# A dense mixture of experts rewritten as a sorted one: every token sent to bins in HBM, 46 slots of 128 rows, answers scattered back

## The chip, the cores and the metric

The kernel runs on one core of one Trainium2 chip. The metric is the device time of one execution in microseconds (us). The kernel before takes 582.26 us, the median of 3 runs.

## The reference

The input is 8 sequences of 256 tokens with 128 features, all float32. Four layers follow each other, and each ends in a residual and a layer norm:

```python
x = _layernorm(x + _L0_attn_ref(x, ...))   # 16 heads, weights (qk)^2-like (a Taylor kernel), causal
x = _layernorm(x + _L0_ffn_ref(x, ...))    # top 1 of 2 experts plus a shared one, hidden 512
x = _layernorm(x + _L1_attn_ref(x, ...))   # 16 heads of 8 with rotary positions, causal softmax
x = _layernorm(x + _L1_ffn_ref(x, ...))    # top 2 of 8 experts, hidden 256
```

The last one is what the change is about:

```python
scores = einsum('bsd,ed->bse', x, Wg)
topk_scores, topk_idx = top_k(scores, 2)
topk_probs = softmax(topk_scores)
h1 = einsum('bsd,efd->bsef', x, W1); h2 = einsum('bsd,efd->bsef', x, W2)
expert_out = einsum('bsef,edf->bsed', silu(h1) * h2, W3)     # all 8 experts for all tokens
out = sum over the two chosen e of topk_probs * expert_out
```

The reference computes all 8 experts for every token and uses two of them.

## The kernel before, in words

Nothing is written in the order in which it runs. The code calls `add` for each operation (a few instructions with the engines that could do them, an estimated cost, and the buffers read and written); `Plan.order` then places all operations by a list schedule with these costs, and the engines' instruction streams follow that order. Each engine works through its own stream in order and waits on semaphores for the others.

The work is cut into stages. `attention0` (stage a) and `attention1` (stage b) run once for each of the 8 sequences, `ffn0` (stage f) and `ffn1` (stage h) once for each of 4 pairs of sequences, 512 tokens. `LIMIT` bounds how many stages of a kind may be open at once, and `STEP`, `LATER`, `WEIGHT` and `WINDOW` set the priorities. All matmuls go through the helper `mm`, so they carry its line, L334, and all copies that of `copy` (L338 on ACT, L340 on DVE).

PSUM has 8 banks: one tile `S` of 4 banks, and 4 single ones. `attention1` fills `S` six times for each sequence: three times with scores whose maximum DVE takes (L982), three times with scores that ACT raises to the exponent (L1028); each filling waits until the one before it has been read. POOL's causal select (L1038) then clears the upper triangle, before the matmuls of attend.

`ffn1` handles 512 tokens with all experts. DVE ranks the 8 gate scores of each token and forms the two gates; they are turned and spread over the partitions (L1183), and the input is multiplied by the gate of each expert (L1189). Then follow 16 chunks (8 experts, two halves of the hidden width): up1, `silu` on ACT (L1208), up2 on the gated input, a product on DVE (L1221), and down into one accumulator. Each chunk has 2 matmuls of 512 columns and 4 of 128. The expert weights `e1`, `e2`, `e3`, 3 MB, are loaded once. The stage ends with a residual (L1238), `layernorm` (L490) and a store by SP.

`layernorm` takes statistics on DVE (L498, L500), the root by a logarithm and an exponential on ACT (L507, L515), and two normalizing operations on POOL or DVE (L522).

Of the kernel before, what the change touches and what calls it, by code (L numbers as in the profile page):

```python
# [10 lines left out]
F32 = mybir.dt.float32  # L11
BF16 = mybir.dt.bfloat16
AF = mybir.ActivationFunctionType
# [3 lines left out]
P = 128  # L17
# [7 lines left out]
E, F = 8, 256  # L25
NEG = -1e30
# [7 lines left out]
for table, parts in (  # L34
# [11 lines left out]
            ("sel8", 1024),  # L46
# [10 lines left out]
def shape_constants():  # L57
# [40 lines left out]
    for j in range(E):  # L98
        part(b, CB, "sel8")[p % 32 == j, 128 * j : 128 * j + 128] = 1.0
# [3 lines left out]
class Buf:  # L103
    def __init__(self, kind, size, name):
        self.kind, self.size, self.name = kind, size, name
        self.slot = None
        self.left = 0
        self.free_at = 0.0
# [9 lines left out]
class Plan:  # L118
# [35 lines left out]
    def order(self, weigh, window=0.12):  # L154
# [8 lines left out]
        slots = {k: [0.0] * n for k, n in self.slots.items()}  # L163
        heap = np.zeros(self.heap)
# [10 lines left out]
        def earliest(b):  # L175
            if b.kind == "heap":
                return room(b.size).min()
            return min(min(slots[k]) for k in b.kind)

        def take(b, t):  # L180
            if b.kind == "heap":
                fit = np.flatnonzero(room(b.size) <= t + 1e-9)
                b.slot = int(fit[0] if b.size > 2 else fit[-1])
                heap[b.slot : b.slot + b.size] = math.inf
                known.clear()
                return
# [6 lines left out]
        def give(b):  # L193
            if b.kind == "heap":
                heap[b.slot : b.slot + b.size] = b.free_at
                known.clear()
            else:
# [83 lines left out]
SLOTS = {"S": 1, "bank": 2, "acc": 2, "vz": 2, "mx": 2, "g4": 2, "small": 40}  # L281
LIMIT = {"a": 4, "f": 4, "b": 2, "h": 3}
HEAP = 160
STEP = {"a": 20.02, "f": 13.515, "b": 17.177, "h": 3.607}
LATER = {"a": -58.15, "f": 14.456, "b": -40.963, "h": 225.772}
WEIGHT = 2.1411
WINDOW = 0.0441
# [3 lines left out]
def network(  # L291
    ctx: ExitStack, tc: tile.TileContext, x, xT, wqk, wv, wo, small, b2, w1, w2, wqkv, wo1,
    e1, e2, e3, ca, cb, out,
# [3 lines left out]
    psum = ctx.enter_context(tc.tile_pool(name="psum", bufs=1, space=bass.MemoryType.PSUM))  # L297
    ctx.enter_context(tc.manual_schedule())

    def fixed(name, shape, dtype=F32):  # L300
        return pool_.tile(shape, dtype, tag=name, name=name)

    banks = [psum.tile([P, 512], F32, tag=f"b{i}", name=f"b{i}") for i in range(4)]
    heap = fixed("heap", [P, HEAP * 256])
    tiles = {
        "S": [psum.tile([P, 4, 512], F32, tag="S", name="S")],
        "bank": banks[2:],
        "acc": banks[:2],
        "vz": [fixed(f"vz_{i}", [P, 1280]) for i in range(SLOTS["vz"])],
        "mx": [fixed(f"mx_{i}", [P, 2, P]) for i in range(SLOTS["mx"])],  # L310
        "g4": [fixed(f"g4_{i}", [P, 4, P]) for i in range(SLOTS["g4"])],
# [3 lines left out]
    def ap(b):  # L315
        if b.kind == "heap":
            return heap[:, b.slot * 256 : (b.slot + b.size) * 256]
        return tiles[b.slot[0]][b.slot[1]]
# [5 lines left out]
    SIZES = {"k8": 8, "k6": 6, "k4": 4, "k2": 2, "k1": 1}  # L324

    def buf(kind, name):
        if kind in SIZES:
            return Buf("heap", SIZES[kind], name)
        if kind == "bank":
            return Buf(("bank", "acc"), 1, name)  # L330
# [140 lines left out]
    for kind, width in (("vz", 1280), ("mx", 256), ("g4", 512)):  # L471
# [18 lines left out]
    def layernorm(tag, r, kind="k1"):  # L490
# [29 lines left out]
        for t in range(2):  # L520
            def apply(e, t=t):
                ENG[e].tensor_scalar(  # L522
                    ap(y)[:, t * P : (t + 1) * P],
# [332 lines left out]

    def attention1(s, xi):
# [240 lines left out]
        return layernorm(f"b{s}", r)  # L1100
# [3 lines left out]
    def ffn1(g, xs):  # L1104
        pt = buf("bank", f"pth{g}")
        xT_ = buf("k2", f"xTh{g}")
        add(f"turn h{g}", pe1(512), transposes(pt, xs), r=both(xs[0]) + both(xs[1]) + ["ca"], w=[pt])
        add(f"turned h{g}", act(512) + dve(512), lambda e: copy(e, ap(xT_), ap(pt)), r=[pt], w=[xT_])
        pg = buf("bank", f"pe{g}")

        def scores(e):
            for t in range(4):
# [5 lines left out]
        add(f"gates {g}", pe(512), scores, r=[xT_, "sml"], w=[pg])  # L1118
        sb = buf("small", f"gs{g}")
        v3 = lambda b, n=E: ap(b)[:, 0 : 4 * n].rearrange("p (t e) -> p t e", t=4)  # L1120
        add(f"gs {g}", act(32) + dve(32), lambda e: copy(e, ap(sb), ap(pg)[:, 0:32]), r=[pg], w=[sb])
        shape = [P, 4, E, E]
        gt, ge = buf("k1", f"gt{g}"), buf("k1", f"ge{g}")
        v4 = lambda b: ap(b).rearrange("p (t a b) -> p t a b", t=4, a=E)
        other = lambda: v3(sb).unsqueeze(2).broadcast_to(shape)
        own = lambda: v3(sb).unsqueeze(3).broadcast_to(shape)
        add(f"gt {g}", dve(256), lambda e: nc.vector.tensor_tensor(v4(gt), other(), own(), ALU.is_gt), r=[sb], w=[gt])
        add(f"ge {g}", dve(256), lambda e: nc.vector.tensor_tensor(v4(ge), other(), own(), ALU.is_ge), r=[sb], w=[ge])
        add(
            f"ge2 {g}", dve(256) + pool(256, True),  # L1130
            lambda e: ENG[e].tensor_mul(
                ap(ge).rearrange("p (t c) -> p t c", t=4),
                ap(ge).rearrange("p (t c) -> p t c", t=4),
                kb("tri8").unsqueeze(1).broadcast_to([P, 4, E * E]),
# [3 lines left out]
        add(f"beats {g}", dve(256), lambda e: nc.vector.tensor_max(ap(gt), ap(gt), ap(ge)), r=[ge], w=[gt])  # L1138
        rank, top, ex, num, den = (buf("small", f"{n}{g}") for n in ("rank", "top", "ex", "num", "den"))
        add(f"rank {g}", dve(256), lambda e: nc.vector.tensor_reduce(v3(rank), v4(gt), AX.X, ALU.add), r=[gt], w=[rank])  # L1140
        add(f"top {g}", dve(32), lambda e: nc.vector.tensor_reduce(v3(top, 1), v3(sb), AX.X, ALU.max), r=[sb], w=[top])
        add(
            f"less {g}", dve(32),
# [221 lines left out]
```

## Time and profile before

| | before |
|---|---|
| median of 3 runs | 582.26 us (580.42 to 582.88) |
| the profiled execution: its time, its span | 582.61 us, 580.9 us |
| instructions in the span | 11773 |
| PE busy | 566.1 us, 97% |
| DVE, ACT, POOL busy | 347.7, 285.4, 80.0 us |
| DMA | 11.99 MB, mean 21 GB/s |

The profile is of one execution. Span is the time from the first to the last instruction. In the groups, a line reads: code line, engine, operation, output and input with their partitions and shape, number of records; then busy time in us and mean ns of one; then the engine's idle time ahead of them and what ended it. A rounded row of digits gives the busy share in tenths in 40 equal slices of the span. PE is TensorE, DVE VectorE, POOL GpSimd, SP the queue that issues DMAs.

### The profile page before, as it was taken

To read this page: it belongs to the slowest core of one execution; us is meant where nothing else is said; L and a number is where in the kernel's file an instruction comes from. 1 tells how busy PE (TensorE), PEld (TensorE's weight loads), DVE (VectorE), ACT (ScalarE), POOL (GpSimd) and SP (SyncE) were. 2 spreads that over 40 slices of the span, in tenths; PEclk is the share of its full clock that TensorE was granted. 3 is DMA by queue.
4 is the path that set the end of the run, shared out by engine and by line. 5 is a ranking of instruction groups with operands and counts; after the bars stand their busy time and mean duration, and the time that the engine had idled before them with its cause. 6 is when DMAs were issued, how large, how long until landed. Compare 5 with 4: busy or idle time off the path is not lost.

```text
span 580.9 us, 11773 instructions
## 1 busy us (share of the span) xinstructions
PE 566.1 (97%) x5146; PEld 370.4 (64%) x5146; DVE 347.7 (60%) x602; ACT 285.4 (49%) x402; POOL 80.0 (14%) x79
## 2 busy tenths in 40 slices
PE   6999999999999999999999999999999999999995
PEld 3666675676666766776666764565565555666674
DVE  2767557655525872777685799757894433513625
ACT  2765666665546535362536358634555322545112
POOL 3000100100000401140424060310301100000100
PEclk9999999999999999999999999999999999999999
DMA  7600000000230000000000000000000000000001
GB/s 279 204 5 1 3 1 1 1 1 1 91 128 2 2 1 2 1 1 3 2 1 2 1 2 3 0 2 1 1 1 1 2 0 0 20 1 1 18 1 37
DMA packets 7433, 11.99 MB, mean 21 GB/s; under 512 B 723, under 2 KB 6102, under 8 KB 6870
## 3 DMA queue, kind: packets, MB, share of 16 engines
q1 hardware_dynamic: 7382, 11.24, 5.7%
q8 instruction: 40, 0.66, 0.5%
q14 instruction: 11, 0.09, 0.1%
HBM read 10.19 MB, written 1.05 MB: 19 GB/s over the span
## 4 chain that ended last, share of the span: by engine, by line
PE 91%; DVE 4%; issue 2%; ACT 1%; POOL 1%; DMA 1%; SPq 0%; DVEq 0%; ACTq 0%; POOLq 0%
PE b L334 73%; PE S L334 17%; PE b L486 1%; DVE heap L910 1%; DMA heap<-in_wqk 1%; ACT L1287 0%; ACT heap L1208 0%; DVE mx L982 0%; DVE heap L876 0%; DVE heap L920 0%; POOL heap L897 0%; DVE heap L1138 0%; DVE heap L522 0%; DVE heap L1221 0%; POOL heap L522 0%
## 5 line engine op out<-in xcount | busy, mean ns | idle before, releaser
L334 PE MATMUL b<-heap 128*128 128x128 f32 (+4 forms) x2272 | 422.4, 358 | 5.3 <-DMA heap<-in_wqk 4.3
L334 PEld LDWEIGHTS b<-heap 128*128 128x128 f32 (+1 forms) x2272 | 267.0, 179 | 127.9 <-issue 82.7
L334 PE MATMUL S<-heap 32*128 32x256 f32 (+1 forms) x1536 | 86.1, 346 | 0.7 <-ACT heap L338 0.7
L334 PEld LDWEIGHTS S<-heap 32*128 32x128 f32 x1536 | 62.4, 186 | 37.5 <-issue 10.0
L1208 ACT ACTIVATE heap<-b 128x512 f32<-128x512 f32 x64 | 37.2, 597 | 88.9 <-PE b L334 88.7
L1221 DVE TENSOR_TENSOR heap<-b,heap 128x512 f32<-128x512 f32 x64 | 43.7, 688 | 60.6 <-PE b L334 60.5
L982 DVE TENSOR_REDUCE mx<-S 128x8 f32<-128x2048 f32 (+1 forms) x24 | 55.0, 2291 | 24.5 <-PE S L334 24.4
L522 POOL TENSOR_SCALAR heap<-heap,sm,sm 128x128 f32<-128x128 f32 x21 | 20.5, 981 | 319.5 <-ACT sm L515 195.1
L338 ACT COPY heap<-b 128x512 f32<-128x512 f32 (+1 forms) x63 | 36.1, 572 | 56.2 <-PE b L334 44.7
L612 ACT ACTIVATE heap<-S,rt_half 128x1536 f32<-128x1536 f32 x32 | 49.2, 1537 | 19.8 <-PE S L334 19.7
L825 ACT ACTIVATE heap<-b,sml 128x512 f32<-128x512 f32 x41 | 28.2, 687 | 60.9 <-PE b L334 60.2
L1028 ACT ACTIVATE heap<-S 128x2048 f32<-128x2048 f32 x24 | 45.1, 1877 | 26.6 <-PE S L334 26.6
L621 DVE SCALAR_TENSOR_TENSOR heap<-heap,ca 128x1024 f32<-128x1024 f32 x32 | 39.1, 1222 | 24.1 <-ACT heap L612 23.1
L1038 POOL TENSOR_SCALAR_AFFINE_SELECT heap<-heap 128x1024 f32<-128x1024 f32 (+1 forms) x24 | 36.8, 1532 | 102.4 <-ACT heap L1028 102.4
L340 DVE COPY heap<-b 128x512 f32<-128x512 f32 (+1 forms) x29 | 18.9, 653 | 37.6 <-PE b L334 26.1
L1287 ACT ACT_TABLE_LOAD x24 | 30.8, 1283 | 0.4
L334 PE MATMUL b<-heap,vz 128*32 128x128 f32 (+1 forms) x512 | 25.8, 330 | 0.9 <-POOL heap L1038 0.6
L733 DVE TENSOR_TENSOR heap<-heap,S 128x1024 f32<-128x1024 f32 x16 | 18.9, 1216 | 5.8 <-PE S L334 5.8
L334 PEld LDWEIGHTS b<-heap,vz 128*32 128x32 f32 x512 | 13.3, 109 | 14.2 <-issue 5.1
L1189 DVE TENSOR_TENSOR heap<-S,heap 128x2048 f32<-128x2048 f32 x8 | 18.3, 2282 | 4.2 <-PE S L334 4.2
L671 ACT ACTIVATE heap<-heap 128x512 f32<-128x512 f32 x28 | 17.6, 630 | 1.5 <-DVE heap L340 0.6
L522 DVE TENSOR_SCALAR heap<-heap,sm,sm 128x128 f32<-128x128 f32 x43 | 14.6, 375 | 5.6 <-ACT sm L515 5.4
(93 smaller groups left out, 315.3 us busy)
## 6 DMA issues: line engine op xcount, KB each, us to landing
heap<-in_e SPq DMA_DIRECT2D x3, 1024.0 KB, 5.9
heap<-in_w SPq DMA_DIRECT2D x2, 768.0 KB, 6.1
cb<-in_cb SPq DMA_DIRECT2D x1, 1332.0 KB, 8.0
heap<-in_xT SPq DMA_DIRECT2D x8, 128.0 KB, 3.2
heap<-in_x SPq DMA_DIRECT2D x8, 128.0 KB, 3.2
out<-heap SPq DMA_DIRECT2D x8, 128.0 KB, 1.9
heap<-in_wv SPq DMA_DIRECT2D x1, 512.0 KB
heap<-in_wo SPq DMA_DIRECT2D x1, 512.0 KB, 5.2
```

The lines of the kernel that those rows point to most:

```text
L334: nc.tensor.matmul(o, l, r, start=start, stop=stop, skip_group_check=True)
L338: nc.scalar.copy(o, i)
L522: ENG[e].tensor_scalar(ap(y)[:, t * P : (t + 1) * P], ap(r)[:, t * P : (t + 1) * P], ap(mv)[:, 2 * t : 2 * t + 1], ap(rs)[:, 2 + t : 3 + t ...
L612: lambda e, sc=sc, atv=atv: nc.scalar.activation(atv(), ap(sc)[:, :, 0:384], AF.Square, bias=rt_half, scale=SQ_SCALE),
L621: lambda e, atv=atv: nc.vector.scalar_tensor_tensor(atv()[:, :, 0:256], atv()[:, :, 0:256], 0.5, ka("tri").unsqueeze(1).broadcast_to([P, 4 ...
L825: nc.scalar.activation(ap(h), ap(ph), AF.Relu, bias=bias)
L982: nc.vector.tensor_reduce(ap(mx)[:, min(part, 1), :].rearrange("p (i j r) -> p i j r", j=4, r=8)[:, :, lo : lo + n, 0], ap(sc).rearrange(" ...
L1028: lambda e, sc=sc, pr=pr: nc.scalar.activation(ap(pr).rearrange("p (i c) -> p i c", i=4), ap(sc), AF.Exp),
L1038: nc.gpsimd.affine_select(out=d, in_=d, compare_op=ALU.is_ge, fill=0.0, base=0, pattern=[[0, 4 * n], [1, P]], channel_multiplier=-1,)
L1208: lambda e, pa=pa, sl=sl: nc.scalar.activation(ap(sl), ap(pa), AF.Silu),
L1221: lambda e, pb_=pb_, sl=sl, h=h: nc.vector.tensor_mul(ap(h), ap(pb_), ap(sl)),
L1287: nc.scalar.preload_act_table_set(table[state])
```

## The change

The second expert network computes only the chosen experts. Stage h is gone, and three new ones stand in its place.

- `route` (stage r, once for each sequence): ranks the gate scores as before, and counts with small bf16 matmuls at which place of which expert's bin each token belongs. `twice` doubles the row, and each copy gets its gate and the number of the row that its answer belongs to (130 columns in all). Four indirect DMAs of POOL (`scatter`) send 128 rows each into bins in HBM. A bin has room for every token.
- `listed` (once for each of two groups of sequences, 0 to 5 and 6 to 7): makes, from the counts, a list of slots. A slot is a tile of 128 rows of one expert. As the counts are known only at run time, there are as many slots as could be needed: 31 for group 0, 15 for group 1.
- `slot` (stage s, 46 times): SP reads two values of the list from SBUF into a register and fetches 128 rows of a bin and the 393 KB of that expert's weights from a table in HBM; PE turns the rows, and up, `silu`, product, down follow for 128 rows; the answer is multiplied by the gate, and one indirect DMA of POOL (`put`) sends the 128 answers to their places. Rows of a bin that hold no token carry numbers of rows that nobody reads.
- `combine` (stage c, once for each sequence): loads the two answers of each token, adds them and the residual, and ends as before.

The bins, 9.5 MB, are cleared at the start by 11 DMAs of SP, with row numbers written by POOL. The PSUM tiles may be shared more freely (`PLACES`: `S` takes banks 0 to 3, kind `any` any of the 8), and the planner's constants are new.

In the built order, attention0 of all sequences stands first, then ffn0 with attention1, then the rest of attention1, and the slots last: the first slot's transpose stands on PE behind the last matmul of attention1 (`wo1` of sequence 7), with the routing of sequence 7 between the first slots. ffn0's last matmul stands ahead of two of the three exponent parts of sequence 4, all three of sequence 5, and all of sequences 6 and 7. On SP all 46 fetches stand ahead of the loads of answers and of the stores; on POOL the scatters stand among the causal selects and the puts behind nearly all of these.

```diff
+GROUPS = ((0, 1, 2, 3, 4, 5), (6, 7))
+ROWS = [len(g) * T for g in GROUPS]
+TILES = [r // P for r in ROWS]
+SLOTN = [2 * t + E - 1 for t in TILES]
+XW = D + 2
...
-SLOTS = {"S": 1, "bank": 2, "acc": 2, "vz": 2, "mx": 2, "g4": 2, "small": 40}
-LIMIT = {"a": 4, "f": 4, "b": 2, "h": 3}
+PLACES = {"S": (0,), "acc": (4, 5), "bank": (4, 5, 6, 7), "any": range(8)}
+SLOTS = {"vz": 2, "mx": 2, "small": 60}
+LIMIT = {"a": 4, "f": 3, "b": 3, "r": 3, "s": 8, "c": 8}
...
-STEP = {"a": 20.02, "f": 13.515, "b": 17.177, "h": 3.607}
-LATER = {"a": -58.15, "f": 14.456, "b": -40.963, "h": 225.772}
-WEIGHT = 2.1411
-WINDOW = 0.0441
+STEP = {"a": 13.636, "f": 36.493, "b": 17.344, "r": 67.492, "s": 2.885, "c": 0}
+LATER = {"a": -290.559, "f": 14.115, "b": -656.553, "r": 89.828, "s": 48.725, "c": 674.472}
+WEIGHT = 2.8227
+WINDOW = 0.0366
...
-    def ffn1(g, xs):
...
+            add(
+                f"clear {g}{a}", [("SP", 0.2 * w, 0.2 * w + 3.0)],
+                lambda e, rows_=rows_, g=g, a=a, w=w: nc.sync.dma_start(
+                    bins[g][a * P : (a + w) * P, :].rearrange("(j p) c -> p j c", p=P),
+                    rows_()[:, 0:w, :],
+                ),
...
+    def route(g, i, st):
...
+        def places(e):
+            o, c = ap(pc), chosen()
+            mm(o[:, 0:16], strict_bf, c, True, False)
+            mm(o[:, 8:16], ones_bf, c[:, 0:8], False, False)
+            mm(o[:, 16:24], ones_bf, c[:, 0:8], False, False)
+            mm(o[:, 16:24], ones_bf, c[:, 8:16], False, True)
...
+                    f"scatter {s}{t}{k}", [("POOL", 1.2, 4.0)],
+                    lambda e, t=t, k=k, n=n: nc.gpsimd.indirect_dma_start(
+                        bin_views[g][n][:, :],
+                        bass.IndirectOffsetOnAxis(
+                            ap=ap(idx)[:, 2 * k + t : 2 * k + t + 1].bitcast(I32), axis=0
+                        ),
+                        rows4(st)[:, t, k, :], None,
+                    ),
+                    r=[(idx, 0), *both(st), (st, "gate"), (st, "dest"), (st, "twice"), *cleared[g]],
...
+    def slot(g, n):
+        tag = f"{g}.{n}"
+        xs_, ws = buf("k1", f"sx{tag}"), buf("k3", f"sw{tag}")
+
+        def fetch(e):
+            rows = ap(lists[g]).bitcast(I32)
+            v = nc.sync.value_load(rows[0:1, n : n + 1], min_val=0, max_val=bins[g].shape[0] - P)
+            nc.sync.dma_start(ap(xs_)[:, 0:XW], bins[g][bass.ds(v, P), :])
+            v = nc.sync.value_load(rows[0:1, 32 + n : 33 + n], min_val=0, max_val=(E - 1) * P)
+            nc.sync.dma_start(ap(ws)[:, 0 : 6 * P], wtab[bass.ds(v, P), :])
+
+        add(
+            f"fetch {tag}", [("SP", 2.0, 5.0)], fetch,
+            r=[lists[g], (lists[g], 1), *scattered[g]], w=[xs_, ws],
+        )
+        pt, xT_ = buf("any", f"st{tag}"), buf("k1", f"sxT{tag}")
+        add(f"turn s{tag}", pe1(128), lambda e: nc.tensor.transpose(ap(pt)[:, 0:P], ap(xs_)[:, 0:P], ident), r=[xs_, "ca"], w=[pt])
+        add(f"turned s{tag}", act(128) + dve(128), lambda e: copy(e, ap(xT_)[:, 0:P], ap(pt)[:, 0:P]), r=[pt], w=[xT_])
+        pu = buf("any", f"su{tag}")
+
+        def up(e):
+            for c in range(4):
+                mm(ap(pu)[:, c * P : (c + 1) * P], ap(ws)[:, c * P : (c + 1) * P], ap(xT_)[:, 0:P], True, True)
...
+        def down(e):
+            for c in range(2):
+                mm(ap(pd)[:, 0:P], ap(h)[:, c * P : (c + 1) * P], ap(ws)[:, (4 + c) * P : (5 + c) * P], c == 0, c == 1)
...
+            f"put s{tag}", [("POOL", 1.2, 4.0)],
+            lambda e: nc.gpsimd.indirect_dma_start(
+                answer_views[g][n][:, :],
+                bass.IndirectOffsetOnAxis(ap=ap(xs_)[:, D + 1 : XW].bitcast(I32), axis=0),
+                ap(yo)[:, 0:P], None,
+            ),
...
+    def combine(g, i, st):
...
+            f"answers {s}", [("SP", 0.5, 3.5)],
+            lambda e: nc.sync.dma_start(
+                ap(yl).rearrange("p (t c) -> p t c", t=2),
+                answers[g][2 * T * i : 2 * T * (i + 1), :].rearrange("(t p k) d -> p t (k d)", t=2, k=2),
+            ),
+            r=answered[g], w=[yl],
...
-    for n, src in (("e1", e1), ("e2", e2), ("e3", e3)):
-        experts[n] = weight(n, src, both(xs[5]))
...
+    for g, members in enumerate(GROUPS):
+        for i, s in enumerate(members):
+            staged("r", s, route, g, i, xs[s])
+        staged("r", members[-1], listed, g)
+        for n in range(SLOTN[g]):
+            staged("s", n + sum(SLOTN[:g]), slot, g, n)
+        for i, s in enumerate(members):
+            staged("c", s, combine, g, i, xs[s])
```

## The prediction

> **What bounds the kernel now.** I read the page's first two parts, then the groups by form, one stretch of the timeline, SP's timeline, and the DMA issues.
>
> ```profile
> PE 566.1 (97%) x5146; PEld 370.4 (64%) x5146; DVE 347.7 (60%) x602; ACT 285.4 (49%) x402; POOL 80.0 (14%) x79
> ...
> PE   6999999999999999999999999999999999999995
> ...
> PEclk9999999999999999999999999999999999999999
> ```
>
> TensorE is busy from end to end at full clock, all other engines have room; only its share can be saved, as long as what remains still fills it.
>
> ```profile
> L334 PE MATMUL b<-heap 128*128 128x512 f32 x416 | 211.8, 615 | 1.0 <-ACT heap L1208 1.0
> L334 PE MATMUL b<-heap 128*128 128x128 f32 x1248 | 165.6, 278 | 0.0
> ...
> L1028 ACT ACTIVATE heap<-S 128x2048 f32<-128x2048 f32 x24 | 45.1, 1877 | 26.6 <-PE S L334 26.6
> ...
> L982 DVE TENSOR_REDUCE mx<-S 128x8 f32<-128x2048 f32 x16 | 36.7, 2293 | 15.0 <-PE S L334 14.9
> ```
>
> The code issues 208 matmuls of 512 columns (128 of them ffn1's) and the group has 416 records: an f32 matmul leaves two. All PE groups of this answer sum to about 644 us where PE is busy 566, so I divide a group's busy time by 1.14. The last two rows are attention1's, for which the one `S` tile is the shared resource.
>
> ```profile
> 471.50 0.69 DVE L1221 TENSOR_TENSOR heap<-b,heap 128x512 f32<-128x512 f32 x1 [3.72 <-PE b L334]
> ...
> 478.59 0.69 DVE L1221 TENSOR_TENSOR heap<-b,heap 128x512 f32<-128x512 f32 x1 [3.74 <-PE b L334]
> ...
> 485.68 0.69 DVE L1221 TENSOR_TENSOR heap<-b,heap 128x512 f32<-128x512 f32 x1 [3.73 <-PE b L334]
> ```
>
> L1221 runs once per chunk of the expert network. The pattern repeats every 7.09 us, three chunks: 2.36 us of PE each, for 1,536 columns.
>
> ```profile
> 1.24 0.42 SPq L359 DMA_DIRECT2D heap<-in_wqk  x1
> 1.70 0.42 SPq L349 DMA_DIRECT2D ca<-in_ca  x1
> 2.17 0.43 SPq L359 DMA_DIRECT2D heap<-in_wv  x1
> ...
> out<-heap SPq DMA_DIRECT2D x8, 128.0 KB, 1.9
> ...
> ca<-in_ca SPq DMA_DIRECT2D x1, 353.0 KB, 3.5
> heap<-in_wqk SPq DMA_DIRECT2D x1, 256.0 KB, 2.9
> ```
>
> SP issues a plain DMA every 0.47 us; 256 to 353 KB land in 2.9 to 3.5 us.
>
> **Removed.** 64 chunks x 2.36 = 151 us of PE, and spread, gate turns, gates and input turns of ffn1: 9.1 + 2.5 + 4.0 + a third of L486's 7.9 = 18.2, by 1.14 = 16. Together 167 of PE's 566; 399 stay. The 3 MB of expert weights were hidden behind PE and bring nothing.
>
> **PE work added.** A slot has 4 up and 2 down matmuls of 128 columns, 12 records at 165.6 / 1248 / 1.14 = 0.117, and a transpose of 7.9 / 48 / 1.14 = 0.145: 1.55 us, 46 slots 71. A sequence's routing is 2 transposes, 2 gate matmuls and 4 tiny bf16 ones, about 1 us, 8 in all. By PE alone the kernel would come to 399 + 71 + 8 = 478 busy, 100 less. The question is what the order lets it keep.
>
> **Until attention1 ends.** The built order puts all of attention0 first, then ffn0 mixed with attention1. ffn0's last matmul stands ahead of 2 scores of sequence 4, 3 of sequence 5 and all 6 of sequences 6 and 7: 17 fillings of `S`, with no other PE work but routing. Attention1's PE groups are two thirds of the `S<-heap` rows (60.0 + 31.8, the rest is attention0's), its `vz` rows 25.7, masks 8.7, 96 records of 128 columns 12.8, a third of the 27.2 of 256 columns, L997 3.1 and a third of L486: 123, by 1.14 = 108, 13.5 a sequence, so this remainder holds 2.9 sequences, 40 us. Before it: 399 - 40 + 5 (five routings) = 364, plus PE's idle 5.0 of the first 50 us, plus 5 that I estimate lost in the mix, where `S` (31 fillings, at the prices below 113 us) stands beside 2.6 groups of ffn0 at 20 and 5.1 sequences at 13.5, 121 us of PE: 374. The remainder goes by `S`: a maximum holds it for its share of PE, (30.6 + 8.7) / 24 / 1.14 = 1.44, 2.29 of L982 and an estimated 0.2 of hops, 3.95; an exponent part 30.6 / 24 / 1.14 = 1.12, 1.88 of L1028 and 0.2, 3.2; 6 x 3.95 + 11 x 3.2 = 59. DVE beside it has two whole sequences at 16.7 (its rows from L876 to L1097 and the layernorm, by sequence), 8 for the others, and 4.5 routings of about 22 small operations, 0.18 to 0.29 each (L1150's 185 ns, L1158's 290), 4.4: 61. Both queues are in order, so I take 65. Attention1 ends at 374 + 65 = **439**, 425 to 452. POOL's scatters stand between the causal selects (L1038) that attend waits for; a scatter that waits for its routing holds the select and so PE. The 5 and the 65 against 59 carry that. Clearing 9.5 MB of bins is ahead of all scatters, behind attention0: nothing. POOL's L522 of sequence 0 stands behind ten index writes that wait for clears, but ffn0 starts only after attention0: nothing; were it sooner, it would cost the clears' length.
>
> **The slots.** Only after sequence 5 is routed can group 0's list be read; its place in PE's order is before the last two exponents of sequence 7, some 14 us ahead of attention1's end, and index, four scatters, their landing (1.9) and 14 list operations take about 12. So fetching starts about with that end, and **nearly all 46 slots stand alone**. Their rate r is that of the slowest queue:
>
> PE 1.55. ACT and DVE about 0.7 each (L1208's and L1221's kinds at half the width or less). DMA moves 393 KB weights, 67 rows in, 64 out: 0.52 MB, at the 279 GB/s of the first slice 1.87 us. POOL issues one indirect put. SP issues two DMAs, 2 x 0.47 = 0.94, and before each a load of a register from SBUF and three register instructions, all in one queue, since each DMA's address needs its load. The trace has no register load. From below it is an event (DVEq's shortest, 0.021), from above a whole DMA's landing (1.9). The nearest rows are round trips of a few bytes: ACT on two elements, L515, 0.20, and that landing; between them (geometric mean) 0.62. Six register instructions at 0.021 are 0.13. r = 0.94 + 2 x 0.62 + 0.13 = **2.31**. At 0.20 SP would need 1.47 and DMA's 1.87 decides; at 1.9, 4.87.
>
> The Trainium skill, "DMA: Bandwidth & Descriptors", section "Latency and other measured facts", gives a register load from memory a floor of about 600 ns; taken as the price, r would be 2.27. No row of this trace shows it.
>
> The put's price is open too: at least an issue of SP's, 0.43; above, L1038's longest kind, 2.1, the costliest POOL row. It decides nothing below 2.31.
>
> The Trainium skill, "SBUF — State Buffer", has a rule against this change: a DMA issued from the POOL queue has its descriptors written by GpSimd, which VectorE can shut out of their shared port; its example goes from about 620 to 3100 ns. If every put paid that, r would be 3.1 and the time 609. The trace has no POOL DMA to weigh it by.
>
> 46 x 2.31 = **106**.
>
> **The end.** After the last fetch is issued, six sequences' answers are loaded by then (2.9), and DVE has 2.3 us for each of two sums, statistics and normalizing: 14 in all, behind the last slots' operations. The last slot itself needs landing 3.5, turn, copy, up, silu, hid, down, gate 4.1 with hops, put and landing 3.2, the answers' load 2.9, two sequences on DVE 4.6 with ACT's 0.5, stores queued on SP, 1.9 to land. With the queues in order, 3.4 + 14 + 4.6 + 1 + 2 = **25**. SP's stores stand behind all fetches; that costs nothing, as no buffer waits for them.
>
> **Sum.** 439 + 106 + 25 = 570 of span. The profiled execution took 582.61 for a span of 580.9, 1.7 around it: 572 in its terms, which lie 0.35 above the median of 582.26, too little to correct. Likeliest: **572**, by 466 + 46 r.
>
> **Rivals.** *SP's chain is dearer*: it eats all of PE's 96 us when r passes (582.6 - 466) / 46 = 2.53, a load of 0.73; measurably slower from 2.59. At a load of 1.0, r = 3.07 and 607. For it: nothing in the old profile covers these waits, and 92 loads stand alone. Against: it needs only a little more than my middle, which is also why it's near. 0.30. *Loads are cheap*: r = 1.87 by DMA, 552; 0.17. *POOL's puts set the rate* at 2.9: 599; needs more than any POOL row of before; 0.07. *Attention1 loses its cover*: the POOL queue or in-order DVE adds 20 us ahead of the slots: 592; 0.06. *It doesn't do what it says*, PE's saving being taken back exactly: about 582; 0.02. Mine, r from 1.97 to 2.58, is 557 to 585: 0.38.
>
> **Chances.** About 0.5%, 3 us, is what a measurement can tell from no change: 579.3 to 585.2. Mine gives 0.33 faster and 0.05 inside; cheap loads are faster. Faster 0.50. Same 0.05 + 0.02 + 0.01 from the slower rivals' near ends, 0.08. Slower 0.42. Range: low, attention1 at 430, r 1.83, an end of 19: 535; high, 452, r 3.15, 27: 624. Since both signs hold much, the likeliest one's own range is 557 to 585.
>
> **What would show it.** PE in the slices should be 9s to about three quarters, then near 6 to the end; its sum 480. The last 110 us should show one slot per 2.3 us, with SP's issues as the pace. Wrong, if issues wait for buffers or puts; if fetching starts well before or after 439; or if the last PE work of attention1 is later than 452.

## The result and the profile after

The changed kernel takes 612.23 us (median of 4 runs, 610.28 to 621.85) against 581.38 for the kernel before on the same chip: a ratio of 1.052, 95% interval 1.047 to 1.056. It is slower, where 572 and a gain were forecast. Ratios, here and below, leave out executions more than 1.5% above the fastest of their kernel, as the 621.85 is. The profiled execution took 613.2 us for a span of 611.5.

First the page: busy time, then the slices of PE and of its granted clock.

```profile
PE 499.6 (82%) x4928; PEld 357.5 (58%) x4928; DVE 327.4 (54%) x727; ACT 256.9 (42%) x437; POOL 170.7 (28%) x186
...
PE   6999699999999999899998987768576677656650
...
PEclk9999799999999999999999888697657587999995
```

PE's work fell from 566 to 500, as it should. But in the last 14 slices, from 397 us on, it is only busy for about six tenths, no engine has taken its place at nine tenths, and the granted clock falls to half in places. Every engine has room in the slots. That is the picture of a chain of waits, not of a slowest queue.

The timeline on PE dates the end of attention1 (`wo1` of sequence 7 is this line of eight records, four matmuls):

```profile
437.56 2.08 PE L369 MATMUL b<-heap 128*128 128x128 f32 x8 [1.08 <-DVE heap L1120]
```

It ends at 439.6; 439 was predicted. SP's timeline has the first fetch at 431.3 and the last at 582.9. So the three parts of the span are:

| | predicted | measured |
|---|---|---|
| until fetching starts | 439 | 431.3 |
| the slots | 46 x 2.31 = 106 | 151.6 (fetches 3.34 apart) |
| from the last fetch to the end | 25 | 28.6 |
| sum | 570 | 611.5 |

The miss lies in the slots; the other two parts together are 4 us shorter than predicted. The busy time in two stretches of them, shown with the granted clock (the third number from the end of a row), goes with two rates: up to 530 the clock is 0.71 and fetches are 3.7 us apart, after 530 it is 1.00 and the pattern repeats every 11.34 us, four slots, 2.84 each. Even at full clock it isn't 2.31.

```profile
431.00:530.00 99.00, 67.11 (x370) 55.17 (x370) 28.62 (x111) 20.00 (x57) 30.89 (x34) 0.71 0.47 143
530.00:583.00 53.00, 34.22 (x246) 28.66 (x247) 13.30 (x37) 12.15 (x36) 17.75 (x19) 1.00 0.60 189
```

### The profile page after: what moved, and what is told of

The parts are those of the page before. It is cut to its first block, busy times and chain, and to the rows that moved or that the text cites. A ratio compares the mean times of both kernels' runs of the same rounds, so it can differ in the third digit from the quotient of the medians.

```text
span 611.5 us, 12538 instructions
## 1 busy us (share of the span) xinstructions
PE 499.6 (82%) x4928; PEld 357.5 (58%) x4928; DVE 327.4 (54%) x727; ACT 256.9 (42%) x437; POOL 170.7 (28%) x186
## 5 line engine op out<-in xcount | busy, mean ns | idle before, releaser
L369 PE MATMUL b<-heap 128*128 128x128 f32 (+4 forms) x1632 | 267.6, 343 | 13.7 <-ACT heap L373 7.3
L369 PEld LDWEIGHTS b<-heap 128*128 128x128 f32 (+1 forms) x1632 | 186.8, 181 | 75.9 <-issue 34.9
L369 PE MATMUL S<-heap 32*128 32x256 f32 (+2 forms) x1960 | 162.1, 351 | 62.0 <-ACT heap L1455 13.8
L369 PEld LDWEIGHTS S<-heap 32*128 32x128 f32 (+1 forms) x1960 | 125.9, 200 | 103.3 <-ACT heap L373 17.0
L1478 POOL DMA_INDIRECT answers<-heap x46 | 44.6, 970 | 98.2 <-DVE heap L1473 33.4
L373 ACT COPY heap<-b 128x512 f32<-128x512 f32 (+2 forms) x73 | 37.6, 516 | 43.5 <-PE b L369 26.5
L659 DVE SCALAR_TENSOR_TENSOR heap<-heap,ca 128x1024 f32<-128x1024 f32 x32 | 39.2, 1226 | 24.8 <-ACT heap L650 24.4
L1455 ACT ACTIVATE heap<-S 128x256 f32<-128x256 f32 x35 | 13.4, 383 | 73.5 <-PE S L369 45.2
L1346 POOL DMA_INDIRECT bins<-heap,sm x32 | 31.7, 991 | 33.4 <-issue 15.7
L1458 DVE TENSOR_TENSOR heap<-S,heap 128x256 f32<-128x256 f32 x35 | 14.6, 421 | 46.4 <-ACT heap L1455 22.9
L375 DVE COPY heap<-b 128x512 f32<-128x512 f32 (+2 forms) x26 | 16.4, 632 | 30.7 <-PE b L369 23.4
L369 PE MATMUL b<-heap,vz 128*32 128x128 f32 (+1 forms) x512 | 29.2, 363 | 1.0 <-POOL heap L1079 0.9
```

The lines of the kernel that those rows point to most:

```text
L369: nc.tensor.matmul(o, l, r, start=start, stop=stop, skip_group_check=True)
L373: nc.scalar.copy(o, i)
L659: lambda e, atv=atv: nc.vector.scalar_tensor_tensor(atv()[:, :, 0:256], atv()[:, :, 0:256], 0.5, ka("tri").unsqueeze(1).broadcast_to([P, 4 ...
L1346: lambda e, t=t, k=k, n=n: nc.gpsimd.indirect_dma_start(bin_views[g][n][:, :], bass.IndirectOffsetOnAxis(ap=ap(idx)[:, 2 * k + t : 2 * k + ...
L1458: add(f"hid s{tag}", dve(256), lambda e: nc.vector.tensor_mul(ap(h), ap(pu)[:, 256:512], ap(sl)), r=[pu, sl], w=[h])
L1478: lambda e: nc.gpsimd.indirect_dma_start(answer_views[g][n][:, :], bass.IndirectOffsetOnAxis(ap=ap(xs_)[:, D + 1 : XW].bitcast(I32), axis= ...
```

## Experiments

Line numbers of the experiments' kernels shown here stand up to seven above those of the changed kernel: the product L1458 is L1465 in e7 and e11, the helper `mm` L369 is L376.

**Four edits on what the prediction named.** e1 takes away the places that fetches wait for. In the changed kernel SP waits much in the slots, most of it for the product of an earlier slot, whose place in the heap the fetch takes. e1 lets the planner give a slot's tiles the place that has been free longest:

```diff
+        self.apart = name[:2] in ("sx", "sw", "ss", "sh", "sy") and "." in name
...
+                if b.apart:
+                    b.slot = int(fit[room(b.size)[fit].argmin()])
```

> Same operations in the same order; only where the slots' buffers lie is changed: each takes the place in the heap that has been free longest, so that a fetch follows the last user of its place by ten slots or more, not four. Theory A (a fetch waits for the product of the slot four before it, a wait made by the placement alone): SP's waits inside the slots vanish, a slot takes SP's own 2.31 us, and the time falls by 46 x (3.30 - 2.31) = 45 us to about 568. Rival B (the slots are as slow as SP's loads and register work make them): under 10 us, 603 or more. Rival C (TensorE's low granted clock in the first 28 slots is the cause, whoever waits): at half clock a slot's matmuls need some 3 us, so about 595, with the clock still low from 440 to 530.

e2 writes the list of slots as constants (those of this input), so that SP loads no register, for the rows as shown and for the weights alike:

```diff
-            v = nc.sync.value_load(rows[0:1, n : n + 1], ...)
+            v = FIXED[g][0][n]
...
```

> The list of slots is written into the code as constants, so SP reads no register; everything else as in the change, the buffers too. It leaves out the reading of the list alone. Theory A: SP still waits for buffers; only the 0.8 us that each load puts into the loop from a product to the next fetch goes, 0.4 to 0.6 us a slot, about 585 to 595. Rival B (SP's register work sets the rate): SP needs about 1 us a slot, the rate falls to DMA's 1.9 or below, 46 x 1.4 = 64 us, about 548.

e3 changes the groups, so that slots can lie beside attention1:

```diff
-GROUPS = ((0, 1, 2, 3, 4, 5), (6, 7))
+GROUPS = ((0, 1, 2, 3), (4, 5, 6, 7))
```

> Groups of sequences 0 to 3 and 4 to 7 in place of 0 to 5 and 6 to 7: still 46 slots, 23 and 23, but the first 23 can run while sequences 4 to 7 are in attention1. If the loss is that nearly all slots stand alone (my step of the prediction), 15 to 20 of them now lie beside attention1, whose S tile left TensorE idle: 50 to 65 us less, 550 to 565. Rival: the slots' operations in the in-order queues hold back attention1 by as much as they are early, so 600 to 615.

e4 adds two idle matmuls ahead of each up and two ahead of each down, into the PSUM tile that these write, to keep PE's clock up:

```diff
+            for _ in range(2):
+                mm(ap(pu)[:, 0:P], ap(ws)[:, 0:P], ap(ws)[:, P : 2 * P], True, True)
...
```

> Two extra matmuls ahead of the ups and two ahead of the downs of each slot, into the tile that the real ones then overwrite: work without use, to keep TensorE busy while it waits. Theory C (the low clock costs 0.7 us in each of the first 28 slots): granted clock near 1.00 from 440 on and about 593. Theory A (the wait for the buffer decides, the clock only lengthens it in part): between 600 and 613; and if the extra matmuls stand in the loop without raising the clock, each slot takes about 0.5 to 1 us more, 635 to 655.

Measured, before at 582.57: e1 621.96 (ratio 1.070, 1.066 to 1.073), e2 622.45 (1.071, 1.065 to 1.076), e3 586.98 (1.009, 1.005 to 1.012), e4 650.51 (1.122, 1.114 to 1.129).

The waits of SP in the slots, of the changed kernel and then of e1 (who waits, for whom: us in total, times, longest):

```profile
SPq L1434 <- DVE heap L1458: 33.1, 20, 6.1
```

```profile
SPq L1439 <- PE b L1446: 4.8, 4, 2.0
```

33.1 us of waits for the product became a few us of others, and the time did not fall. These waits were a consequence: SP stood behind a chain that was slow anyway. In e1 SP runs ahead of the slots: its fetches are 2.57 us apart where they were 3.34, but the puts, one for each finished slot, repeat every 11.34 us for four slots at full clock, as in the changed kernel and in e2. So the spacing of fetches is the rate of the slots only as long as SP has to wait for them. e2 gains nothing either, so SP's register loads aren't the pace. Neither SP's own issues nor its waits for places explain the slow slot; POOL's puts, which the prediction named too, are answered further below. e4 costs 38 us: 8 more records of 0.117 in each of 46 slots are 43, so almost every microsecond that is put into a slot's accesses is paid, though PE stands idle a third of the time: at full clock four slots take 14.66 us there for 11.34. And the clock is up, at 0.94 up to 530, where the changed kernel has 0.71:

```profile
437.00:530.00 93.00, 63.82 (x494) 55.79 (x494) 26.97 (x104) 18.12 (x52) 27.84 (x31) 0.94 0.44 136
```

So a higher clock alone does not make the slots fast. e3 gains 25 us, with slots beside attention1, and says nothing on the rate.

**A deeper order.** The next theory was that the planner believes in latencies that are too short, so that only one or two slots are under way. e6 adds 0.8 us to the assumed latency of six steps and lets 12 slots be open; the instructions stay, their order becomes down n, turn n+4, up n+3.

```diff
+def late(alts):
+    return [(e, b, l + 0.8) for e, b, l in alts]
...
-        add(f"up s{tag}", pe(512), up, r=[xT_, ws], w=[pu])
+        add(f"up s{tag}", late(pe(512)), up, r=[xT_, ws], w=[pu])
...
-LIMIT = {"a": 4, "f": 3, "b": 3, "r": 3, "s": 8, "c": 8}
+LIMIT = {"a": 4, "f": 3, "b": 3, "r": 3, "s": 12, "c": 8}
...
```

> In the changed kernel the 46 slots take 3.37 us each where SP's own issues need 2.31, and neither SP's waits for places (e1) nor its register loads (e2) were the cause. Here the planner is told that the turn, the copy, the up, the silu, the product and the down of a slot end 0.8 us later than it assumed, and up to 12 slots (8 before) may be open; nothing else changes, and every instruction is the same. The order on TensorE becomes down n, turn n+4, up n+3, where it was up n, turn n+1, down n-1 or closer. Theory of the latency chain (each slot's turn, copy, up, silu, product and down follow one another across three engines, with one or two slots under way, so all engines wait for one another, and TensorE's gaps let the granted clock fall): 46 slots at 2.3 to 2.6 us instead of 3.37, so 35 to 50 us less, 562 to 578 us, with the granted clock of the slots above 0.85. Theory of the queue of DMAs (the fetches and the puts move no faster than one slot per 2.8 us at any order): 600 to 612 us. Theory that the granted clock falls whatever the order, since TensorE is busy under two thirds: slots at 2.9 us or more while the clock is at half, 590 to 605 us.

e7 is e6 with e1's places, e9 is e7 with e2's constants, e8 is e7 with e3's groups.

> The same deeper order, and the slots' tiles at the place that has been free longest (e1), so that SP's fetches do not wait for a product that is now further behind. Theory of the latency chain: SP is then the slowest queue at its own 2.31 us per slot, 439 + 106 + 27 = 572 us and a little under e6 if the deeper order makes fetches wait there. Theory of the queue of DMAs or of the clock: as e1, 600 to 622 us.

> As e7, with the list of the slots written as constants, so that SP issues two DMAs per slot and loads no register (e2). If SP's 2.31 us per slot bound e7, this is faster by up to 0.4 us per slot (down to the DMA engines' 1.87): 552 to 565 us, 7 to 20 us below e7. If the slots of e7 still go by the compute chain or by the clock, both are equal within 3 us.

> As e7, with the second network's batches as two groups of four sequences instead of six and two, so that the first 23 slots can lie beside attention of the last four. e3 (the groups alone) took 587 us. Theory of the latency chain: the 23 slots left behind attention take 2.3 to 2.5 us instead of over 3 and the sum falls by 15 to 25 us, to 560 to 572 us, below the kernel before. Theory of the queue of DMAs or of the clock: 583 to 590 us.

Measured, before at 580.63: e6 649.40 (1.121, 1.115 to 1.128), e7 643.61 (1.097, 1.091 to 1.103), e9 650.82 (631.47 to 654.32, no interval), e8 597.19 (1.027, 1.023 to 1.031). With slots further apart in the order the kernel got slower: by their ratios e6 and e7 by 40 and 26 us against the change, e8 by 10 against e3, whose groups it has, and e9, at its fastest, by 9 against e2. None of my theories had that. So a slot's steps wait for something else than their own inputs. The timeline of e7 says for what:

```profile
481.25 0.27 ACT L380 COPY heap<-S 128x128 f32<-128x128 f32 x1 [2.46 <-PE S L376]
...
481.55 0.42 DVE L1465 TENSOR_TENSOR heap<-S,heap 128x256 f32<-128x256 f32 x1 [1.10 <-ACT heap L380]
```

The product (L1465) needs the up and the silu of its slot. It waits for a copy (L380), which makes the turned rows of another slot. Both read `S`. e6 shows the same over all its slots: its 34 products out of `S` have 40.7 us of idle DVE ahead of them, 24.8 of these ended by such a copy.

**The shared tile.** `PLACES` lets the slots' PSUM tiles (kind `any`) lie in any of 8 banks, and the planner takes the bank that was freed last. In the changed kernel 106 of the 138 tiles of the slots (35 turns, 35 ups, 36 downs, counted in the trace; the 109 in e16's expectation is a miscount) fall into banks 0 to 3. For the planner these are four banks; in the program they are one tile, `S`. The program holds every access to `S` until the last access of another engine to `S`, at whatever bank. For slots 40 and 41 the waits are:

```
turn 41     (PE,  bank 0)  waits for silu 40    (ACT, bank 1)
product 40  (DVE, bank 1)  waits for turn 41    (PE,  bank 0)
copy 41     (ACT, bank 0)  waits for product 40 (DVE, bank 1)
up 41       (PE,  bank 0)  waits for copy 41    (ACT, bank 0)
```

Only the last of the four is a need of the data. The changed kernel's timeline shows the four steps one after the other, from the silu of slot 40 to the up of slot 41:

```profile
576.55 0.38 ACT L1455 ACTIVATE heap<-S 128x256 f32<-128x256 f32 x1 [1.27 <-PE S L369]
...
576.99 0.33 PE L1443 MATMUL S<-ca,heap 128*128 128x128 f32 x1
...
577.35 0.42 DVE L1458 TENSOR_TENSOR heap<-S,heap 128x256 f32<-128x256 f32 x1 [1.61 <-PE S L1443]
...
577.81 0.27 ACT L373 COPY heap<-S 128x128 f32<-128x128 f32 x1 [0.45 <-DVE heap L1458]
...
578.13 0.60 PE L369 MATMUL S<-heap 128*128 128x128 f32 x3 [0.81 <-ACT heap L373]
```

The groups of the changed kernel, shapes kept apart, show the price in one kernel, since some slots lie in `S` and some in `b` (the columns after the bar: busy us, mean ns, then the idle time of the engine ahead of them and who ended it):

```profile
L1458 DVE TENSOR_TENSOR heap<-S,heap 128x256 f32<-128x256 f32 x35 | 14.6, 421 | 46.4 <-ACT heap L1455 22.9 <-PE S L1443 21.2 <-PE S L369 2.3
...
L1471 ACT ACTIVATE heap<-S,heap 128x128 f32<-128x128 f32 x13 | 4.8, 367 | 11.3 <-DVE heap L1458 4.9 <-PE S L369 4.7 <-DMA heap<-answers 1.7
L1458 DVE TENSOR_TENSOR heap<-b,heap 128x256 f32<-128x256 f32 x11 | 4.6, 422 | 0.1
...
L1471 ACT ACTIVATE heap<-b,heap 128x128 f32<-128x128 f32 x10 | 3.7, 367 | 0.5
```

35 products out of `S` have 46.4 us of idle DVE ahead of them, 21.2 of these ended by a turn (L1443), which no product needs; 11 products out of `b` have 0.1. The 22.9 ended by a silu can be each product's own need. The gate on ACT is alike: 11.3 against 0.5. A second stretch at full clock shows how one slot holds the next:

```profile
549.25 0.38 ACT L1455 ACTIVATE heap<-S 128x256 f32<-128x256 f32 x1 [2.37 <-PE S L369]
549.66 0.42 DVE L1458 TENSOR_TENSOR heap<-S,heap 128x256 f32<-128x256 f32 x1 [2.13 <-ACT heap L1455]
...
550.12 0.37 ACT L1471 ACTIVATE heap<-S,heap 128x128 f32<-128x128 f32 x1 [0.49 <-DVE heap L1458]
...
550.54 0.71 PE L369 MATMUL S<-heap 128*128 128x128 f32 x4 [1.22 <-ACT heap L1471]
```

The gate of one slot (L1471) starts when the product of the next has ended, and that slot's down starts when the gate has ended: silu, product, gate, down, one at a time, on three engines that are all free. Such a chain should be longer the more the slots are interleaved. That this is why e6 to e9 lost is inferred, but e11 below bears it out: e7's order without `S` takes about 60 us less than e7 (ratios 0.992 and 1.097).

The Trainium skill, "PSUM — Partial Sum Buffer", section "PSUM bank collisions raise a hardware error", says that two different engines may not touch one bank in the same partitions at the same time, reads included, and advises to guard PSUM by bank rather than by address. This program guards by tile, and `S` is four banks. No run here takes a guard away, so none shows what it prevents; the runs below show what it costs to guard four banks as one.

e10 confines the slots' tiles to banks 4 to 7, four tiles of their own; the order of the work stays, but for a few of the first slots and one gate that goes from DVE to ACT, as in e16 too.

```diff
-        pt, xT_ = buf("any", f"st{tag}"), buf("k1", f"sxT{tag}")
+        pt, xT_ = buf("bank", f"st{tag}"), buf("k1", f"sxT{tag}")
...
-        pu = buf("any", f"su{tag}")
+        pu = buf("bank", f"su{tag}")
...
-        pd = buf("any", f"sd{tag}")
+        pd = buf("bank", f"sd{tag}")
```

> The slots' PSUM tiles (turn, up, down) were given any of eight banks, and the planner, which takes the bank freed last, put most of them into banks 0 to 3. Those four banks are one tile of the program (S, the attention scores' tile), and the waits in the traces say that every access of a slot to S is held until the last access of another engine to S, whatever the bank: a product of one slot waits for the copy of another, a silu for another slot's turn. Here the slots' tiles are confined to banks 4 to 7, four tiles of their own; the order of work, the groups and all else stay. Theory of the shared tile (the slots go one access at a time through S, so their latencies add): the slots go at 2.3 to 2.7 us each instead of 3.37 and the time falls by 30 to 45 us, to 567 to 582 us; the waits left are those of a slot on itself and on a reused bank. Theory of the clock (TensorE's granted clock falls in the slots whatever they wait for): no gain, 605 to 622 us. Theory that the four banks, too few, bring new waits: 612 us or more.

e11 is e10 with e7's order and places, e13 is e11 with e3's groups.

> e10 with the deeper order of e7 (down n beside up n+5 and turn n+7) and the slots' tiles in the heap at the place free longest. With S this order was worse than the change itself (649 and 644 us for e6 and e7). Theory of the shared tile: without S the deeper order hides the hops between the engines, SP's 2.31 us per slot is all that is left, 439 + 106 + 27 = 572 us, within 555 to 578. Theory of the clock: TensorE, busy about 60 %, is still granted half of the clock in part of the slots, 600 us or more.

> e11 with the batches as two groups of four sequences, e8 (597 us) without S in the slots. Theory of the shared tile: 23 slots lie beside attention1 of the last four sequences and 23 come after it at 2.31 us each: 60 us after about 450 to 460 us and an end of 27, so 540 to 555 us, below the kernel before (581). Theory of the clock: 585 to 597 us.

e16 is the control to e10, the same edit with banks 0 to 3:

```diff
-PLACES = {..., "any": range(8)}
+PLACES = {..., "any": range(8), "quad": (0, 1, 2, 3)}
...
-        pt, xT_ = buf("any", f"st{tag}"), buf("k1", f"sxT{tag}")
+        pt, xT_ = buf("quad", f"st{tag}"), buf("k1", f"sxT{tag}")
...
-        pu = buf("any", f"su{tag}")
+        pu = buf("quad", f"su{tag}")
...
-        pd = buf("any", f"sd{tag}")
+        pd = buf("quad", f"sd{tag}")
```

> The control to e10: the slots' PSUM tiles are again confined to four banks, but to banks 0 to 3, which are the one tile S. In the changed kernel 79 in 100 of the slots' tiles lie there (109 of 138; the others in bank 4). Theory of the shared tile: with every access in S the chain through it is unbroken, so each slot takes the sum of its six accesses and their hops, 3.5 to 4.2 us, and the time is 615 to 650 us. Theory that e10 gained by something else, such as the choice of four fixed banks: 575 to 585 us, as e10.

| slots' PSUM tiles | time (us) | ratio, 95% interval | between fetches (us) |
|---|---|---|---|
| e16: all in `S` | 681.89 | 1.170, 1.165 to 1.175 | 4.55 |
| the change: 106 of 138 in `S` | 612.23 | 1.052, 1.047 to 1.056 | 3.34 |
| e10: none, same order | 578.74 | 0.996, 0.993 to 0.998 | 2.53, the last 34 at 2.37 |
| e11: none, deeper order | 576.59 | 0.992, 0.989 to 0.995 | 2.44 |

Four banks in `S` and four banks outside differ by 103 us. That the slots pass through one tile is shown, by both signs; the number of banks isn't it. The product's row in e16 says the same, with nearly all of its idle time ended by a turn:

```profile
L1458 DVE TENSOR_TENSOR heap<-S,heap 128x256 f32<-128x256 f32 x46 | 19.2, 420 | 76.8 <-PE S L1443 72.1 <-ACT heap L1455 3.1 <-PE S L369 1.6
```

e16 is dearer than I expected (615 to 650). The clock stays low too, at 0.54 up to 530 and 0.67 to 648; its share of the 682 is not separated. Its timeline over one slot at half clock:

```profile
603.89 2.90 PE L369 MATMUL S<-heap 128*128 128x128 f32 x12 [1.18 <-ACT heap L1455]
...
606.87 0.38 ACT L1455 ACTIVATE heap<-S 128x256 f32<-128x256 f32 x1 [3.74 <-PE S L369]
...
607.31 0.33 PE L1443 MATMUL S<-ca,heap 128*128 128x128 f32 x1 [0.52 <-ACT heap L1455]
...
607.68 0.42 DVE L1458 TENSOR_TENSOR heap<-S,heap 128x256 f32<-128x256 f32 x1 [3.89 <-PE S L1443]
608.14 0.37 ACT L1471 ACTIVATE heap<-S,heap 128x128 f32<-128x128 f32 x1 [0.88 <-DVE heap L1458]
608.40 0.26 ACT L373 COPY heap<-S 128x128 f32<-128x128 f32 x1
...
608.71 1.60 PE L369 MATMUL S<-heap 128*128 128x128 f32 x12 [1.07 <-ACT heap L373]
```

Matmuls, silu, turn, product, gate, copy and the next matmuls follow each other without overlap: 4.82 us from one up to the next. The 12 records of up and down take 2.90 us here at half clock and 1.60 at full clock.

In e10 the product's row has changed sides. All 46 are out of `b`, no turn ends their idle time, and the silu (L1455) ends nearly all of it:

```profile
L1458 DVE TENSOR_TENSOR heap<-b,heap 128x256 f32<-128x256 f32 x46 | 19.3, 424 | 33.6 <-ACT heap L1455 31.5 <-DMA answers<-heap 1.7
```

**What sets the pace without the shared tile.** SP's and PE's timelines of e11, with the fetches and a turn (L1450):

```profile
499.42 0.33 SPq L1441 DMA_DIRECT2D heap<-bins  x1
...
499.86 0.30 PE L1450 MATMUL b<-ca,heap 128*128 128x128 f32 x1 [0.81 <-DMA heap<-bins]
...
500.60 0.34 SPq L1443 DMA_DIRECT2D heap<-in_wtab  x1
```

An issue follows the other by 1.14 to 1.18 us, and PE's turns now wait for the rows to land: 23.0 us of idle PE ahead of the 46 turns. To see whether SP's issues are the pace, e15 is e11 with e2's constants. To use the answer without constants, e17 is e13 with the weights' fetch, its register load included, on ScalarE's queue:

```diff
-            v = nc.sync.value_load(rows[0:1, 32 + n : 33 + n], ...)
-            nc.sync.dma_start(ap(ws)[:, 0 : 6 * P], wtab[bass.ds(v, P), :])
+        def fetch_w(e):
+            v = nc.scalar.value_load(rows[0:1, 32 + n : 33 + n], ...)
+            nc.scalar.dma_start(ap(ws)[:, 0 : 6 * P], wtab[bass.ds(v, P), :])
...
```

> e11 (slots outside S, deeper order, places apart; 577 us, fetches 2.44 us apart) with the list of slots as constants, so that SP loads no register. e2 and e9 did the same while S set the rate and gained nothing. Theory that SP's own issues (2.31 us per slot) bound e11, as the prediction had it: the rate falls toward the DMA engines' and TensorE's 1.6 to 1.9 us per slot, 46 x 0.4 = 18 us less, 553 to 565 us. Theory that DMA transfers or the compute chain already bind at 2.4: within 4 us of e11.

> e13 (two groups of four, slots outside S, deeper order; 555 us) with the weights of a slot fetched from ScalarE's queue, register load included, so that SP has one fetch per slot (1.16 us) and ScalarE 0.7 + 1.16 us. Theory that SP's issues bound the 23 slots that come after attention: they go at 1.9 to 2.1 us instead of 2.4, 7 to 11 us less, 543 to 549 us. Against it: a weight fetch that waits for its place in ScalarE's queue holds the silus behind it, and in the first 23 slots it holds attention's exponentials: then 555 to 570 us.

e15 takes 556.83 (0.957, 0.954 to 0.959), 20 us less than e11, with puts 1.73 us apart where e11 has 2.29. Its fetches are 1.85 apart in the mean. The same edit had brought nothing while `S` set the rate (e2, e9). The stretches of e15 have the share of the DMA engines in the number before the last:

```profile
465.00:485.00 20.00, 16.44 (x135) 15.32 (x136) 8.44 (x26) 5.75 (x18) 11.20 (x12) 1.00 1.02 366
485.00:505.00 20.00, 18.53 (x162) 17.96 (x161) 8.21 (x24) 6.65 (x23) 11.79 (x13) 1.00 0.96 308
```

The DMA engines are full in both, and PE is busy for 93% of the second. From 505 to 527 the DMA share is 0.41 and PE is busy for 89%. So e11 was bound by SP, and beneath SP lie first the DMA engines and then PE, close together.

e17 takes 569.30 (0.981, 0.974 to 0.987), 14 us more than e13, within the range of the case against it. Its weights' fetches go every 1.5 us from 482 to 505 and every 2.0 from 510 to 531. But ScalarE's operations stand behind earlier fetches (a copy at 408 had 7.2 us of idle ScalarE ahead of it, ended by a weights' DMA), and ScalarE issues no fetch at all from 425.8 to 458.9: its stream, in order, has attention1's last exponents there, layer norms, routing and the silus of slots already fetched. Whether those fetches also wait for a place is not shown.

e13 takes 555.18 (0.956, 0.952 to 0.959; 554.17 to 556.88). It is the fastest kernel here that works for any input, 27 us under the kernel before and 57 under the change.

## Why the prediction was wrong, step by step

**The step that failed** is "Their rate r is that of the slowest queue". SP, the slowest queue, was costed rightly, but r is the slowest queue's only if the slots overlap freely, and the working never asked whether the tiles of different slots can be held at the same time. It knew `S` as the resource that serializes attention1 ("the one `S` tile is the shared resource"), and the diff lets the slots' tiles lie in banks 0 to 3; the two were not put together. r was 3.34 in place of 2.31: 151.6 us for 106. e10 takes back 33.5 of the 40 us between the prediction and the result with this one cause removed, and e11 lands at 577 beside the 572.

At full clock the chain through `S` is worth 2.84 - 2.31 = 0.53 a slot, 24 us for 45 intervals. The other 45 x (3.34 - 2.84) = 22 us lie up to 530, where the clock is 0.71, but this stretch also holds attention1's last 8 us and the start of the slots, whose first put comes 28 us after the first fetch. By the puts, 3.02 apart, only 45 x (3.02 - 2.84) = 8 us are left there. What the clock costs of that is not shown. e4 had the clock up and its puts 3.60 apart, but its idle matmuls lie in the chain, so it shows that the clock alone is not the cause and not what it costs. In e10 the same stretch has 0.91. That the clock falls because of the chain is not shown either, and e11 and e15 still have short stretches at half clock.

**SP's price held.** Two issues of SP without a wait between them are 1.15 us apart, as in the changed kernel's stretch at full clock:

```profile
548.83 0.33 SPq L1436 DMA_DIRECT2D heap<-in_wtab  x1
549.98 0.33 SPq L1434 DMA_DIRECT2D heap<-bins  x1
```

That is 2.30 a slot for a sum of 2.31. Less the 0.47 of a plain issue, a load with its register instructions is 0.68; 0.685 was put down. The middle of so wide a bracket (0.20 to 1.9) could as well have been off; that it fits is luck. Without loads, e15's first five slots are fetched 0.85 to 0.95 us apart, two plain issues each. The Trainium skill, "DMA: Bandwidth & Descriptors", section "Latency and other measured facts", gives 600 ns for the load, and the estimate with it was 2.27; these rows cannot separate the load from what follows it, and agree with both.

**DMA's price was too high, and the 1.85 of e15 agrees with its 1.87 by luck.** The 279 GB/s were read off a slice in which the DMA engines were not full, the first of this row (busy tenths, 7):

```profile
DMA  7600000000230000000000000000000000000001
```

In e15 they are full at 308 to 366 GB/s, and the first 42 fetches, 443.5 to 502.5, are 1.44 us apart. The mean of 1.85 contains 15.4 us, 507.0 to 522.4, in which SP issues nothing; the next on its queue is a load of answers. The term did not set r, so the sum has nothing of this, but the 1.87 of *Loads are cheap* was too long: e15's puts are 1.73 apart.

**Attention1's end, 439.6 for 439, came out by two misses that cancel.** The working has 374 us until ffn0's last matmul and 65 for the remainder. But the sum that reads ffn0's last result (L886) starts at 357.2, and the last exponent part ends at 429.1:

```profile
357.19 0.76 DVE L886 TENSOR_TENSOR heap<-b,heap 128x256 f32<-128x256 f32 x2
```

```profile
427.21 1.88 ACT L1069 ACTIVATE heap<-S 128x2048 f32<-128x2048 f32 x1 [0.84 <-POOL heap L1079]
```

So the first part is 17 us shorter and the remainder, 82 us, is 17 longer: its 17 fillings of `S` take 72 us where 59 were summed, and 10.5 us follow the last of them (attend, routing, `wo1`), for which there was no term. PE is busy for 338 us in the first part, where 364 were put down, and for 59 in the remainder, where about 43 were, at a clock of 0.80. Why the split is so different is not shown. The scatters are a small part of it: of the 11 selects of the remainder, two start 0.2 and 0.6 us after their exponent, behind a scatter, and the others within 0.1 us. Fetching began 8 us ahead of attention1's end, within the 14 that the prediction saw. Two small slips change nothing: 1.44 + 2.29 + 0.2 is 3.93 and not 3.95, and the upper end of the range, 624, lacks the 1.7 us that the lower one has.

**The end** is 28.6 for 25 as a whole; its terms are not told apart here. PE's busy time is 500 for 480; 12 records take 1.8 times as long at half clock.

**The rivals.** POOL's puts were priced between 0.43 and 2.1. The group of L1478 has the shortest, median and longest in ns:

```profile
L1478 POOL DMA_INDIRECT answers<-heap x46: 963/967/1044, 459.2 to 595.2; - x46
```

No put took 2.9. The Trainium skill, "SBUF — State Buffer", section "A bandwidth-pool intuition that's wrong (but worth ruling out)", has an example in which VectorE shuts GpSimd out and makes such a DMA five times as long: none of the 46 puts shows it, with DVE busy 41.9 of the 152 us. Whether DVE ever ran an instruction of the kind that the page means beside a put, no run here shows. "SP's chain is dearer" has the right size, 607, by the wrong cause. That r could pass 2.53 by a chain from slot to slot was not among the rivals, and "wrong, if issues wait for buffers or puts" pointed at a consequence: the issues did wait, and e1 took the waits away for nothing.

## What to carry to other kernels

A stage goes at the rate of its slowest queue only if nothing ties its iterations to each other, so ask of each pair of neighbours which buffer they both touch, and at what granularity the program guards it: a tile that spans several banks is one resource, whatever a planner takes it for. When every engine of a stage has room, look for waits that the data don't need (a product that waits for a transpose); comparing the same instruction on two tiles within one trace points to them before any experiment. If a deeper order makes a kernel slower, as here by 26 to 40 us, look for a resource that its iterations share. And a sum that comes out right is no proof of its terms: 439 was right by two misses, 1.87 by a pause.

## What the runs showed of the hardware that I had not expected

The granted clock fell to 0.50 while PE was never idle for long: from 450 to 480 in the changed kernel PE's longest gap is 1.55 us and it is busy for about two thirds, yet the clock is at 0.50 for about 19 of the 30 us, and after 530 the same pattern runs at 1.00. What decides between the two these runs don't show. An indirect DMA of 128 rows held POOL for 0.96 to 1.04 us in all 46 puts. The DMA engines, full, moved 366 GB/s in e15's 465 to 485.
